# Rounds of eight edge tiles instead of batches of four in a graph-attention kernel

## The chip, the cores and the metric

One core of a Trainium2 chip. The metric is the device time of one execution in microseconds (us); lower is better. Engines: PE (matrix), DVE (vector), ACT (scalar), POOL (here it only issues gathers) and SP (issues plain transfers).

## The reference

A graph with 6250 nodes and 206250 edges, sorted by destination, with 128 features in 8 heads of 16:

```python
Qh, Kh, Vh = (h @ W).reshape(N, 8, 16)   # for WQ, WK, WV
Eh = (edge_attr @ WE).reshape(-1, 8, 16)
score = einsum('ehd,ehd,ehd->eh', Kh[src], Qh[dst], Eh) / sqrt(16)
score = exp(clip(score, -5, 5))
wV = segment_sum(Vh[src] * score[:, :, None], dst)
Z = segment_sum(score, dst)
out = layernorm(x + wV / (Z + 1e-6))
```

## The kernel before

Edges are cut into 1612 tiles of 128, one edge to a partition, and tiles into batches of four. A first stage makes a table of K and V rows (`kv`, in DRAM). Then 406 batches run through a software pipeline; the order of the instructions on each engine is the order in which the Python code issues them (a scheduler only arranges the first twelve batches).

- **Gathers (L397, POOL).** One indirect DMA for each tile fetches 128 rows of K and V by source node. The first gather of a batch carries a dependency on a matmul of an earlier batch (`expanded[b - lag(b)]`, lag from 12 batches down to 3), so that gathers keep PE's pace; the others of the batch have none.
- **Columns (L352 to L370).** For 141 tiles the rows are not gathered. ACT (104 source nodes) and DVE (24) copy the nodes' columns of x, 4 bytes in each of 128 partitions, from `xT_sb` into a tile `xcol`, one instruction for each column, its address taken from a register; a register load (L365) fetches eight addresses at once. PE projects the tile (L379), DVE puts the result in the place of the gathered rows (L386). The copies are spread over the batches by a due count (`columns`): one column tile in 2.6 batches.
- **Scores.** PE expands Q rows by a one-hot matrix (`qps`, L448) and projects edge features (`eps`, L453), one PSUM bank each. DVE multiplies K by Q (`kq`, L459), by E (`kqe`, L462), reduces by head (`sc`, L465) and clips (L468). ACT takes the exponential twice, into PSUM for DVE (`exp_p`, L474) and beside the messages (`msg`, L476). DVE multiplies V by it (L503).
- **Sums.** PE adds messages and weights into a window of 128 nodes by another one-hot matrix (`agg`, L525); two batches share a window, and two windows a PSUM tile, which ACT copies out once per four batches (`sum`, L535). Windows are shifted into blocks of 128 nodes (`finps`, L488), ACT copies these (`fin`, L498), and DVE normalizes.
- **Order in iteration b.** PE's Q and E for b; gathers; half of ACT's columns; DVE: kq(b-1), one-hot(b+2), kqe(b-1), turned one-hot(b+2), reduce(b-1), messages(b-2), DVE's columns, clip(b-1); ACT: exponentials(b-1), the rest of its columns; PE: sums(b-2).

Of the kernel before, what the change touches and what calls it, by code (L numbers as in the profile page):

```python
# [16 lines left out]
P = 128  # L17
# [3 lines left out]
B = 4  # L21
G = 4
HW = 64
HALF = 16
# [4 lines left out]
CH = 8  # L29
GB = 14  # L30
XB = 12
LOCK = XB + 6
STEP = 3
GLEAD = 2
OHB = (3, 5)
# [5 lines left out]
AHEAD = 2  # L41
EB = 6
SLAG = 2
# [8 lines left out]
COL0 = 32  # L52
COLP = (13, 5)
COLA = (8, 13)
COLV = (8, 3)
COLL = 8
RING = 4096
SUMS = 8
# [4 lines left out]
def cut_batches():  # L63
    out, t = [], 0
    while t < NT:
        k = B
        if t >= NT - TAIL:
            k = 2 if NT - t > 3 else 1
        out.append(range(t, t + k))
        t += k  # L70
    return out
# [9 lines left out]
def pair_of(t):  # L81

    return (t // (2 * G), t // G % 2) if t < LAST else (NT, 1)


def pair_start(k):

    return (2 * k * G * N + NT // 2) // NT - DRIFT


def window_start(t):
    k, half = pair_of(t)
    return QL * P + HW if k == NT else pair_start(k) + HALF * half
# [8 lines left out]
def edge_attention(ctx: ExitStack, tc: tile.TileContext, x, xT, srcT, srcC, dstT, dstB, dst0, bnd, lo, eaT,  # L102
# [26 lines left out]
    halves = [[cp.tile([P, B, P], F32, name=f"onehot{h}{i}") for i in range(OHB[h])] for h in range(2)]  # L129
# [11 lines left out]
    with ExitStack() as fast:  # L141
# [8 lines left out]
        nc.vector.tensor_scalar(shift[:HW], io_i[:HW], 0, None, op0=ALU.is_equal)  # L150
        nc.vector.tensor_scalar(shift[HW:], io_i[HW:], HALF - HW, None, op0=ALU.is_equal)
        nc.vector.tensor_scalar(ident, io_i[:, P:2 * P], 0, None, op0=ALU.is_equal)
        for h in range(2):
            for tl in halves[h]:
                nc.vector.memset(tl[:, :, HW - HW * h:P - HW * h], 0.0)
# [85 lines left out]
        psA = fast.enter_context(tc.tile_pool(name="psA", bufs=2, space=bass.MemoryType.PSUM))  # L241
        psX = fast.enter_context(tc.tile_pool(name="psX", bufs=1, space=bass.MemoryType.PSUM))

        iota_p = psX.tile([P, HW], F32, name="iota_p")
        exp_p = psX.tile([P, B, H], F32, name="exp_p")
# [33 lines left out]
        xbs, stores, norms, pending, ready, finished, loaded_x = {}, [], [], [], [], [], set()  # L279
# [39 lines left out]
        def load_rel(c):  # L319
            if c in rels or c * RC >= NT:  # L320
                return
            n = min(RC, NT - c * RC) * P
            rels[c] = wp.tile([QROWS, RC * P], BF16, name="relb", bufs=2)
# [3 lines left out]
        chunks, aggs, sums, st8, expanded = {}, {}, {}, {}, {}  # L327
# [20 lines left out]
        used = [0, 0]  # L348
# [59 lines left out]
        def project(g, n):  # L408

            pt = psT.tile([P, B, P], F32, name="xtps", tag="oT")  # L410
            for i in range(n):
                nc.tensor.transpose(pt[:, i, :], g[:, i, :D], ident)
            xgT = wp.tile([P, B, P], F32, name="xgT", tag="kq", bufs=2)
            nc.scalar.copy(xgT[:, :n], pt[:, :n])
            for i in range(0, n, 2):
                k = min(2, n - i)
                pk = pair_bank(i // 2, "kvps", [P, 2, 2 * D])
                for j in range(k):
                    nc.tensor.matmul(pk[:, j, :], xgT[:, i + j, :], wkv_sb, start=True, stop=True)  # L419
                nc.scalar.copy(g[:, i:i + k, :], pk[:, :k, :])  # L420

        def stage_0(b):
            t0, n = batches[b][0], len(batches[b])
            half = pair_of(t0)[1]
            oh = halves[half][used[half] % OHB[half]]
            used[half] += 1
            nc.vector.tensor_tensor(oh[:, :n, HW * half:HW * half + HW],  # L427
                                    iota_p[:, None, :].to_broadcast([P, n, HW]),
                                    rel[:, t0:t0 + n, None].to_broadcast([P, n, HW]), op=ALU.is_equal)
            st8[b] = oh, None  # L430

        def stage_0t(b):
            t0, n = batches[b][0], len(batches[b])
            oh = st8[b][0]
            ohT = wp.tile([QROWS, B * P], BF16, name="onehotT", bufs=AHEAD + 2)
# [3 lines left out]
            st8[b] = oh, ohT  # L439

        def stage_a(b, g):
            t0, n = batches[b][0], len(batches[b])
            if b < XB:
                project(g, n)
            oh, ohT = st8.pop(b)
            pq = psQ.tile([P, B, D], F32, name="qps")
            for i in range(n):
                expanded[b] = nc.tensor.matmul(pq[:, i, :], ohT[:, i * P:i * P + P], loaded[t0 // WT],  # L448
                                               start=True, stop=True)
            pe = psE.tile([P, B, D], F32, name="eps")  # L450
            ea = ea_tiles(t0, n)
            for i in range(n):
                nc.tensor.matmul(pe[:, i, :], ea[:, i * P:i * P + P], we_sb, start=True, stop=True)  # L453
            st8[b] = [n, g, oh, pq, pe]

        def stage_b(b):
            n, g, oh, pq, pe = st8[b]
            t0 = wp.tile([P, B, D], F32, name="kq", bufs=2)
            nc.vector.tensor_tensor(t0[:, :n], g[:, :n, :D], pq[:, :n], op=ALU.mult)  # L459
            yield  # L460
            t1 = wp.tile([P, B, D], F32, name="kqe", bufs=2)
            nc.vector.tensor_tensor(t1[:, :n], t0[:, :n], pe[:, :n], op=ALU.mult)  # L462
            yield
            sc = wp.tile([P, B, H], F32, name="sc")
            nc.vector.tensor_reduce(sc[:, :n], t1[:, :n].rearrange("p b (h d) -> p b h d", h=H),  # L465
# [3 lines left out]
            st8[b] = [n, g, oh, sc]  # L469

        def weigh(b):

            n, g, oh, sc = st8[b]
            nc.scalar.activation(exp_p[:, :n], sc[:, :n], AF.Exp, scale=0.25)  # L474
            m = wp.tile([P, B, MW], F32, name="msg")
            nc.scalar.activation(m[:, :n, D:], sc[:, :n], AF.Exp, scale=0.25)  # L476
            st8[b] = [n, g, oh, m]

        def windows(q):

            return [(k, pair_start(k) - q * P) for k in range(min(NT, LAST + 2 * G - 1) // (2 * G))
                    if -HW - HALF < pair_start(k) - q * P < P]

        def add_windows(ps, q, first, stop):

            parts = windows(q)
            for i, (k, s) in enumerate(parts):
                nc.tensor.matmul(ps, shift[:, P - s:2 * P - s], sums[k // 2][:, k % 2],  # L488
# [12 lines left out]
        def messages(b):  # L501
            n, g, oh, m = st8[b]
# [5 lines left out]
        def stage_c(b):  # L508
            n, g, oh, m = st8.pop(b)
            for i in range(n):  # L510
                t = batches[b][i]
                k, half = pair_of(t)
# [5 lines left out]
                u = k if final else k // 2  # L518
                first = u not in aggs
                if first:  # L520
                    aggs[u] = psA.tile([P, 2, MW], F32, name="agg")
                    if final:
                        add_windows(aggs[u][:, 0], QL, True, False)
                tail = k == NT if t == NT - 1 else pair_of(t + 1)[0] != k
                nc.tensor.matmul(aggs[u][:, 0 if final else k % 2], oh[:, i, :], m[:, i, :],  # L525
                                 start=not final and t % (2 * G) == 0, stop=tail)
                if tail and final:
                    norms.extend(pending)
# [3 lines left out]
                    norms.append(layernorm(nc, sp, aggs.pop(u)[:, :1], xbs.pop(QL), out, QL, 1, stores))  # L532
                elif tail and (k % 2 == 1 or t == LAST - 1):
                    sums[u] = sp.tile([P, 2, MW], F32, name="sum", bufs=SUMS)
                    nc.scalar.copy(sums[u][:, :k % 2 + 1], aggs.pop(u)[:, :k % 2 + 1])  # L535
                    while len(finished) < QL // 2 and all(v // 2 <= u for v, _ in windows(2 * len(finished) + 1)):
                        ready.append(len(finished))
                        finished.append(u)

        gathered = {b: gather(b) for b in range(2)}  # L540
        for b0 in range(0, NB, KB):
# [3 lines left out]
            for b in range(len(gathered), min(XB, nbat)):  # L545
                if (b - 2 if b < 5 else b) * KB > b0:
                    break
# [6 lines left out]
        load_rel(0)  # L554
        for j in range(QLOOK):
            load_q(j)

        def fill():

            if qwork:  # L560
# [5 lines left out]
        for b in range(nbat + 3):  # L566
# [6 lines left out]
            if b < nbat:  # L573
                load_chunk(batches[b][0] // CH + EB - 3)
                load_rel(batches[b][0] // RC + 1)
                load_q(batches[b][0] // WT + QLOOK)
                g = gathered.pop(b)
                if b == min(XB, nbat - 1):
                    late_loads()
                if b == min(XB + 8, nbat - 1):  # L580
                    relative(C0, NT)
                if b == 14:
                    from_window(1)
                if b == 0:
                    for i in range(AHEAD):
                        stage_0(i)
                        stage_0t(i)
                stage_a(b, g)
# [3 lines left out]
            norms.extend(pending)  # L592
# [4 lines left out]
            steps = stage_b(b - 1) if 0 <= b - 1 < nbat else iter(())  # L597
            next(steps, None)
            if b + AHEAD < nbat:
                stage_0(b + AHEAD)  # L600
            fill()
            next(steps, None)
            place_columns()
            if b + AHEAD < nbat:
                stage_0t(b + AHEAD)
            fill()
            next(steps, None)
            if 0 <= b - 2 < nbat:
                messages(b - 2)
# [181 lines left out]
```

## Time and profile before

| | us |
|---|---|
| median of 3 runs | 2546.33 (2535.9 to 2577.7) |
| the profiled execution | 2564.92 |
| its span | 2563.1 |
| first column copies to last, about | 250 to 2500 |

In the profile a line such as "L370 ACT COPY xcol<-xT_sb 128x4 uint8 x14664 | busy, mean ns | idle <-releaser" is a group of equal instructions: the time in which one of them runs, the mean of one, and the idle time of the engine just before them with what ended it. "issue" means that nothing the profile shows was waited for. A row of the waits reads: total us, times, longest. A row of the timeline reads: start, duration, engine, line, and in brackets the idle time before it. A row of a window reads: from and to, its length, then busy us and instruction count of each engine, then PE's granted clock, the DMA engines' share and GB/s. "remote" is a wait that a DMA's landing ended. Instructions on an engine overlap: a small copy takes 190 ns from start to acknowledged end, and the next may start 95 ns after it.

### The profile page before, as it was taken

What the parts mean: (1) busy time and instruction counts of PE and PEld (TensorE: products, weight loads), DVE (VectorE), ACT (ScalarE), POOL (GpSimd) and SP (SyncE); (2) the same over time, 40 slices, a digit from 0 to 9 for tenths busy, and PEclk for the clock granted to TensorE, in tenths of its full rate; (3) what the DMA queues carried; (4) which work ended last, traced back from release to release, by engine and by line L of the source; (5) the groups of instructions that cost most, each with busy time, mean ns of one, the idle gap of its engine ahead of it and who ended that gap; (6) DMA issues with size and microseconds to landing.
All of it is one profiled execution on the core that took longest, in us unless ns stands there. A gap on an engine that the chain in (4) does not pass through costs nothing.

```text
span 2563.1 us, 49459 instructions
## 1 busy us (share of the span) xinstructions
PE 1618.7 (63%) x9332; PEld 1406.9 (55%) x9332; DVE 1757.4 (69%) x7175; ACT 1700.3 (66%) x15663; POOL 1398.5 (55%) x1478
## 2 busy tenths in 40 slices
PE   4665555566665666666656566666666666666666
PEld 3554455455555556555555555555555565555555
DVE  2365666777767767777767677677676777767776
ACT  1221667677776777777767777777776777777771
POOL 5455445555555555555555555455555555555554
PEclk7687778776877877787777778877777677777777
DMA  6555434455455446445545454454455545545542
GB/s 204 178 157 165 136 119 148 139 164 156 135 152 162 131 132 191 131 150 156 152 147 146 144 162 129 141 176 134 136 155 156 151 131 163 163 130 150 155 144 79
DMA packets 171260, 381.43 MB, mean 149 GB/s; under 512 B 58733, under 2 KB 84645, under 8 KB 170943
## 3 DMA queue, kind: packets, MB, share of 16 engines
q0 software_dynamic: 69824, 189.69, 25.6%
q1 hardware_dynamic: 99979, 187.45, 24.1%
q14 instruction: 240, 1.97, 0.3%
q8 instruction: 77, 1.26, 0.2%
q10 hardware_dynamic: 1140, 1.06, 0.1%
HBM read 363.26 MB, written 14.81 MB: 148 GB/s over the span
## 4 chain that ended last, share of the span: by engine, by line
ACT 48%; issue 23%; DVE 9%; PE 8%; ACTq 7%; another core or an unknown queue 3%; DMA 1%; POOL 0%; DVEq 0%; SPq 0%; POOLq 0%
ACT xcol L370 44%; ACTq L365 7%; PE agg L525 2%; PE eps L453 2%; ACT msg L476 2%; DVE kqe L462 1%; DVE xcol L370 1%; DVE kq L459 1%; ACT exp_p L474 1%; DVE msg L503 1%; DVE sc L465 1%; PE kvps L419 1%; PE finps L488 1%; ACT sum L535 1%
## 5 line engine op out<-in xcount | busy, mean ns | idle before, releaser
L397 POOL DMA_INDIRECT kvrows<-kv,src x1423 | 1352.1, 950 | 1116.1 <-PE qps L448 382.1
L370 ACT COPY xcol<-xT_sb 128x4 uint8 x14664 | 1560.9, 190 | 557.3 <-issue 544.4
L525 PE MATMUL agg<-msg,onehot 128*128 128x136 f32 x3224 | 635.5, 356 | 561.2 <-DVE msg L503 406.9
L525 PEld LDWEIGHTS agg<-msg,onehot 128*128 128x128 f32 x3224 | 551.5, 250 | 621.9 <-ACT msg L476 383.2
L453 PE MATMUL eps<-we_sb,ea 128*128 128x128 f32 x3224 | 607.0, 346 | 195.6 <-DVE kqe L462 67.0
L453 PEld LDWEIGHTS eps<-we_sb,ea 128*128 128x128 f32 x3224 | 528.0, 248 | 252.9 <-DVE kqe L462 96.4
L503 DVE TENSOR_TENSOR msg<-kvrows,exp_p 128x512 f32<-128x512 f32 x406 | 275.8, 679 | 415.6 <-ACT exp_p L474 262.7
L370 DVE COPY xcol<-xT_sb 128x4 uint8 x3384 | 301.7, 194 | 16.9 <-issue 10.8
L459 DVE TENSOR_TENSOR kq<-kvrows,qps 128x512 f32<-128x512 f32 x406 | 274.2, 675 | 40.7 <-remote 24.7
L462 DVE TENSOR_TENSOR kqe<-kq,eps 128x512 f32<-128x512 f32 x406 | 273.7, 674 | 26.6 <-remote 18.2
L465 DVE TENSOR_REDUCE sc<-kqe 128x32 f32<-128x512 f32 x406 | 272.1, 670 | 0.3
L448 PE MATMUL qps<-qw,onehotT 126*128 126x128 bf16 x1612 | 200.1, 259 | 84.3 <-DVE kq L459 47.8
L448 PEld LDWEIGHTS <-onehotT 126*128 126x128 bf16 x1612 | 159.5, 120 | 153.6 <-issue 130.5
L427 DVE TENSOR_TENSOR onehot<-iota_p,dst_sb 128x256 f32<-128x256 f32 x406 | 167.9, 414 | 2.4 <-PE agg L525 2.4
L437 DVE TENSOR_SCALAR onehotT<-relb,node 126x512 bf16<-126x512 bf16 x406 | 146.3, 361 | 5.8 <-PE qps L448 2.6
L474 ACT ACTIVATE exp_p<-sc 128x32 f32<-128x32 f32 x406 | 78.0, 192 | 107.6 <-DVE sc L468 57.2
L386 DVE COPY kvrows<-colkv 128x256 f32<-128x256 f32 x141 | 59.5, 422 | 87.9 <-PE eps L453 26.3
L379 PE MATMUL colkv<-wkv_sb,xcol 128*128 128x256 f32 x282 | 115.3, 501 | 0.0
L488 PE MATMUL finps<-sum,shift 128*128 128x136 f32 x640 | 93.1, 305 | 32.7 <-ACT sum L535 29.0
L488 PEld LDWEIGHTS finps<-sum,shift 128*128 128x128 f32 x640 | 88.3, 213 | 35.7 <-ACT sum L535 31.7
L476 ACT ACTIVATE msg<-sc 128x32 f32<-128x32 f32 x406 | 86.9, 214 | 7.1 <-issue 6.6
L468 DVE TENSOR_SCALAR sc<-sc 128x32 f32<-128x32 f32 x406 | 81.8, 202 | 0.3
(72 smaller groups left out, 562.6 us busy)
## 6 DMA issues: line engine op xcount, KB each, us to landing
ea<-eaT SPq DMA_DIRECT2D x201, 512.0 KB
relb<-relD SPq DMA_DIRECT2D x100, 504.0 KB
kvrows<-kv,src POOLq DMA_INDIRECT x1423
qw<-qs SPq DMA_DIRECT2D x202, 31.5 KB
kv<-kvst SPq DMA_DIRECT2D x12, 512.0 KB
qs<-qst SPq DMA_DIRECT2D x48, 96.0 KB
xb<-x SPq DMA_DIRECT2D x24, 128.0 KB
out<-h SPq DMA_DIRECT2D x24, 128.0 KB
```

The source lines that it names most:

```text
L365: at = nc.values_load_multi_w_load_instructions(col_at[k % col_half:k % col_half + 1, k // col_half, j:j + size], engines=(engine,), min_v ...
L370: copy(to[:, 4 * (j + c):4 * (j + c) + 4], xT_bytes[:, ds(at[c] - XT_AT, 4)])
L397: ins = nc.gpsimd.indirect_dma_start(out=g[:k, i, :f], out_offset=None, in_=rows, in_offset=bass.IndirectOffsetOnAxis(ap=src_col(t)[:k], a ...
L427: nc.vector.tensor_tensor(oh[:, :n, HW * half:HW * half + HW], iota_p[:, None, :].to_broadcast([P, n, HW]), rel[:, t0:t0 + n, None].to_bro ...
L448: expanded[b] = nc.tensor.matmul(pq[:, i, :], ohT[:, i * P:i * P + P], loaded[t0 // WT], start=True, stop=True)
L453: nc.tensor.matmul(pe[:, i, :], ea[:, i * P:i * P + P], we_sb, start=True, stop=True)
L459: nc.vector.tensor_tensor(t0[:, :n], g[:, :n, :D], pq[:, :n], op=ALU.mult)
L462: nc.vector.tensor_tensor(t1[:, :n], t0[:, :n], pe[:, :n], op=ALU.mult)
L465: nc.vector.tensor_reduce(sc[:, :n], t1[:, :n].rearrange("p b (h d) -> p b h d", h=H), axis=AX.X, op=ALU.add)
L488: nc.tensor.matmul(ps, shift[:, P - s:2 * P - s], sums[k // 2][:, k % 2], start=first and i == 0, stop=stop and i == len(parts) - 1)
L503: nc.vector.tensor_tensor(m[:, :n, :D].rearrange("p b (h d) -> p b h d", h=H), g[:, :n, D:].rearrange("p b (h d) -> p b h d", h=H), exp_p[ ...
L525: nc.tensor.matmul(aggs[u][:, 0 if final else k % 2], oh[:, i, :], m[:, i, :], start=not final and t % (2 * G) == 0, stop=tail)
```

## The change

Batches become rounds of eight tiles (206 instead of 406). Each round's Q and E are made and used in two halves of four tiles, with two PSUM banks for each (they come from `agg`, which goes from two banks to one, and from putting the one-hots' iota and the exponentials into one). Reduction, clip, both one-hots, exponentials and messages are done for eight tiles at once. The sums' window spans sixteen tiles instead of eight, with the one-hot written at one of four offsets; ACT copies one window out per two rounds. Column tiles come one per 1.25 rounds: 144 of them, with eight addresses to a load as before. kq and kqe of a half follow each other on DVE, kqe in place. The one-hot for the sums is made in its own round, ahead of the clip, from a ring of three. Gathers: eight per round, buffers for 8 rounds (14 batches before), first gather of a round tied to the matmul `lag` rounds before (6 down to 2).

```diff
-B = 4
+B = 8
-GB = 14
-XB = 12
+GB = 8
+XB = 6
-STEP = 3
-GLEAD = 2
+STEP = 2
+GLEAD = 1
-COLP = (13, 5)
+COLP = (5, 4)
...
-        psE = fast.enter_context(tc.tile_pool(name="psE", bufs=1, space=bass.MemoryType.PSUM))
-        psQ = fast.enter_context(tc.tile_pool(name="psQ", bufs=1, space=bass.MemoryType.PSUM))
+        psE = fast.enter_context(tc.tile_pool(name="psE", bufs=2, space=bass.MemoryType.PSUM))
+        psQ = fast.enter_context(tc.tile_pool(name="psQ", bufs=2, space=bass.MemoryType.PSUM))
...
         def lag(b):
-            return max(STEP, 12 - (b - LOCK) // 40)
+            return max(STEP, 6 - (b - LOCK) // 20)
...
+            nc.vector.tensor_tensor(t0[:, a:e], g[:, a:e, :D], pq[:, :k], op=ALU.mult)
             yield
+            nc.vector.tensor_tensor(t0[:, a:e], t0[:, a:e], pe[:, :k], op=ALU.mult)
...
+        def take_sums():
+            for k in closed:
+                sums[k] = sp.tile([P, MW], F32, name="sum", bufs=SUMS)
+                nc.scalar.copy(sums[k], agg[:, k % 2])
...
+            for _ in stage_b(b, 0):
+                fill()
+            stage_a(b + 1, 0)
+            fill()
+            take_sums()
+            if 0 <= b - 1 < nbat:
+                messages(b - 1)
+            fill()
+            place_columns()
+            if b < nbat:
+                columns(nc.vector, b, 0.5)
+            for _ in stage_b(b, 1):
+                fill()
+            stage_a(b + 1, 1)
+            if 0 <= b - 1 < nbat:
+                stage_c(b - 1)
+            steps = stage_s(b) if b < nbat else iter(())
             next(steps, None)
+            turned_one_hots(b + 2)
+            if b < nbat:
+                one_hots(b)
             fill()
             next(steps, None)
+            if b < nbat:
+                weigh(b)
             fill()
             if b < nbat:
                 columns(nc.vector, b)
+                columns(nc.scalar, b)
```

`stage_a` is PE's Q and E for a half, `stage_b` DVE's two products, `stage_s` reduction and clip, `weigh` the exponentials, `stage_c` PE's sums. ACT's other half of the columns of round b stands ahead of all this.

More of the change, by code (lines that the diff above doesn't have):

```diff
@@ L408, in project @@
         def project(g, n):
[L410 to L420, printed above, removed]
@@ L422, in stage_0 @@
-        def stage_0(b):
+            for a in range(0, n, G):
+                h = min(G, n - a)
+                pt = psT.tile([P, G, P], F32, name="xtps", tag="oT")
+                for i in range(h):
+                    nc.tensor.transpose(pt[:, i, :], g[:, a + i, :D], ident)
+                xgT = wp.tile([P, G, P], F32, name="xgT", tag="kvst", bufs=2)
+                nc.scalar.copy(xgT[:, :h], pt[:, :h])
+                for i in range(0, h, 2):
+                    k = min(2, h - i)
+                    pk = psT.tile([P, 2, 2 * D], F32, name="kvps", tag="oT")
+                    for j in range(k):
+                        nc.tensor.matmul(pk[:, j, :], xgT[:, i + j, :], wkv_sb, start=True, stop=True)
+                    nc.scalar.copy(g[:, a + i:a + i + k, :], pk[:, :k, :])
@@ L456, in stage_b @@
[L456 to L459, printed above, removed]
-            yield
[L461 to L465, printed above, removed]
+            st8[b] = [ohT]
@@ new lines, in half, with stage_a @@
+        def half(b, h):
+            return range(h * G, min(len(batches[b]), h * G + G)) if 0 <= b < nbat else range(0)
+        def stage_a(b, h):
+            own = half(b, h)
+            if not own:
+                return
+            if b < XB and h == 0:
+                project(gathered[b], len(batches[b]))
+            t0, ohT = batches[b][0], st8[b][0]
+            pq = psQ.tile([P, G, D], F32, name="qps")
+            for i in own:
+                expanded[b] = nc.tensor.matmul(pq[:, i - own[0], :], ohT[:, i * P:i * P + P], loaded[t0 // WT],
+                                               start=True, stop=True)
+            pe = psE.tile([P, G, D], F32, name="eps")
+            ea = ea_tiles(t0, len(batches[b]))
+            for i in own:
+                nc.tensor.matmul(pe[:, i - own[0], :], ea[:, i * P:i * P + P], we_sb, start=True, stop=True)
+            st8[b].append((pq, pe))
@@ L517, in stage_c @@
                 final = k == NT
[L518 to L526, printed above, removed]
-                if tail and final:
-                    norms.extend(pending)
+                u = (LAST - 1) // (QUAD * G) + 1 if final else k
+                if final and t == LAST:
+                    take_sums()
+                    add_windows(agg[:, u % 2], QL, True, False)
+                tail = t == NT - 1 or window_of(t + 1)[0] != k
+                nc.tensor.matmul(agg[:, u % 2], oh[:, i * P + HW - at:][:, :P], m[:, i, :],
+                                 start=not final and t % (QUAD * G) == 0, stop=tail)
+                if tail and final:
+                    for j in ready:
+                        finish(j)
+                    ready.clear()
+                    norms.extend(waiting + pending)
+                    waiting.clear()
                     pending.clear()
@@ L531, in stage_c @@
                         fill()
[L532 to L540, printed above, removed]
+                    norms.append(layernorm(nc, sp, agg[:, u % 2:u % 2 + 1], xbs.pop(QL), out, QL, 1, stores))
+                elif tail:
+                    closed.append(k)
+        def take_sums():
+            for k in closed:
+                sums[k] = sp.tile([P, MW], F32, name="sum", bufs=SUMS)
+                nc.scalar.copy(sums[k], agg[:, k % 2])
+                while len(finished) < QL // 2 and all(v <= k for v, _ in windows(2 * len(finished) + 1)):
+                    ready.append(len(finished))
+                    finished.append(k)
+            closed.clear()
+        gathered = {0: gather(0)}
         for b0 in range(0, NB, KB):
@@ L565, in edge_attention @@
         held = []
-        for b in range(nbat + 3):
+        for b in range(nbat + 2):
+            now[0] = b
             if b >= XB and not manual:
```

174 lines of the change are left out of this document (79 added, 95 removed).

## The prediction

> **What bounds the kernel now.** I began with the page: span, busy shares, and the chain of work that ended last.
>
> ```profile
> span 2563.1 us, 49459 instructions
> PE 1618.7 (63%) x9332; PEld 1406.9 (55%) x9332; DVE 1757.4 (69%) x7175; ACT 1700.3 (66%) x15663; POOL 1398.5 (55%) x1478
> ACT 48%; issue 23%; DVE 9%; PE 8%; ACTq 7%; another core or an unknown queue 3%; DMA 1%; POOL 0%; DVEq 0%; SPq 0%; POOLq 0%
> L397 POOL DMA_INDIRECT kvrows<-kv,src x1423 | 1352.1, 950 | 1116.1 <-PE qps L448 382.1
> L370 ACT COPY xcol<-xT_sb 128x4 uint8 x14664 | 1560.9, 190 | 557.3 <-issue 544.4
> ```
>
> By busy shares nothing is full (DVE leads with 69%), but the chain runs through ACT and "issue". ACT's column copies (L370) keep it busy 1560.9 us, and before them it idles another 557 us, 544 of which waited for no other engine. So I asked what ACT waits for in the stretch in which columns are copied (about 250 to 2500 us), and how busy the engines are there.
>
> ```profile
> ACT xcol L370 <- issue: 544.1, 1008, 1.2
> ACT exp_p L474 <- issue: 13.9, 22, 1.2
> ACT exp_p L474 <- DVE sc L468: 5.2, 4, 3.7
> ACT fin L498 <- PE finps L488: 4.9, 3, 2.7
> ACT sum L535 <- PE agg L525: 1.1, 1, 1.1
> 250.00:2500.00 2250.00, 1427.61 (x8291) 1248.09 (x8291) 1598.88 (x6756) 1651.41 (x15497) 1231.85 (x1297) 0.77 0.50 148
> ```
>
> The last row gives PE, weight loads, DVE, ACT and POOL. ACT is busy 1651 us and held up in issue 570 (544.1, 13.9 and two rows of 6.6 and 5.9): 2222 of 2250 us. It waits for DVE and PE some 11 us in all. ACT is full; everyone else waits for it. The 570 us are worth understanding, so I laid POOL's timeline beside ACT's.
>
> ```profile
> 1072.70 0.94 POOL L397 DMA_INDIRECT kvrows<-kv,src  x1 [1.87 <-remote]
> 1075.20 0.95 POOL L397 DMA_INDIRECT kvrows<-kv,src  x1 [0.30 <-issue]
> ...
> 1080.30 0.95 POOL L397 DMA_INDIRECT kvrows<-kv,src  x1 [0.30 <-issue]
> 1086.40 0.95 POOL L397 DMA_INDIRECT kvrows<-kv,src  x1 [5.16 <-DVE kqe L462]
> ```
>
> ```profile
> 1072.65 0.19 ACT L474 ACTIVATE exp_p<-sc 128x32 f32<-128x32 f32 x1
> 1072.78 0.21 ACT L476 ACTIVATE msg<-sc 128x32 f32<-128x32 f32 x1
> 1072.90 2.51 ACT L370 COPY xcol<-xT_sb 128x4 uint8 x24
> 1075.32 0.38 ACT L535 COPY sum<-agg 128x272 f32<-128x272 f32 x1
> 1075.59 0.95 ACT L370 COPY xcol<-xT_sb 128x4 uint8 x9
> 1076.94 0.38 ACT L370 COPY xcol<-xT_sb 128x4 uint8 x3 [0.39 <-issue]
> 1077.71 0.19 ACT L370 COPY xcol<-xT_sb 128x4 uint8 x1 [0.38 <-issue]
> ...
> 1081.25 0.38 ACT L370 COPY xcol<-xT_sb 128x4 uint8 x3 [0.50 <-issue]
> 1082.67 3.52 ACT L370 COPY xcol<-xT_sb 128x4 uint8 x36 [1.04 <-issue]
> ```
>
> A train of seven gathers, 1.25 us apart, starts at 1072.70; its third gather starts at 1075.20. ACT copies at 0.1 us each (24 in 2.51 us) until shortly after that, then 1 to 3 copies between gaps of 0.4 to 1.0 us. The train's last gather ends at 1081.25; from 1082.67 ACT runs free, 36 copies in 3.52 us. I read the stalls as belonging to the third and later gathers of a train. Trains of other lengths test that; these are ACT's issue waits within three windows.
>
> ```profile
> ACT xcol L370 <- issue: 1.7, 2, 1.1
> ACT xcol L370 <- issue: 4.1, 8, 1.0
> ACT xcol L370 <- issue: 5.1, 9, 1.1
> ```
>
> They are a train of four (1091.0 to 1097.1 us), the seven above (1072.7 to 1086.4) and a train of eight (1579.1 to 1594.4). Per gather past the second: 1.7/2 = 0.85, 4.1/5 = 0.82, 5.1/6 = 0.85. The law 0.84 x (n - 2) can be held against the whole stretch: POOL's timeline there has 335 trains with 1295 gathers, so 1295 - 670 = 625 gathers past the second, 525 us; measured 544. Short trains are nearly free now because each batch of four tiles opens its own: POOL's first gather of a batch waits for PE.
>
> [...]
>
> **The change, part by part.** Counts for the changed kernel come from its built instruction list.
>
> *Trains of gathers.* POOL now waits once per round of eight tiles; the instruction list has one wait for PE and DVE ahead of the first gather, then 8 gathers, or 7 where a column tile takes the place of one. 144 column tiles (141 before) lie in about 180 rounds: 144 trains of seven and 36 of eight. Stalls: 144 x 4.1 + 36 x 5.1 = 774 us against 544: **+230**. This is the main term. [...] These rows hold ACT's column copies alone:
>
> ```profile
> 1072.70:1086.40 13.70, 8.80 (x82) 0.50 0.25 71
> 1579.10:1594.40 15.30, 8.52 (x79) 0.77 0.46 140
> ```
>
> A round copies 104 x 0.8 = 83 columns, what these windows hold. At 13.7 us with seven gathers and 15.3 with eight, 180 rounds take 144 x 13.7 + 36 x 15.3 = 2524 us for the stretch's 2250: +274.
>
> *Column copies.* 14976 instead of 14664: 312 x 0.106 us (1560.9/14664) = **+33**, on ACT, on the path.
>
> *Exponentials.* 206 pairs instead of 406, 64 elements wide instead of 32. A pair costs 0.25 us (1072.65 to the copy at 1072.90). An element costs what wide copies differ by:
>
> ```profile
> L414 ACT COPY xgT<-xtps 128x512 f32<-128x512 f32 x12 | 7.0, 584 | 37.5 <-remote 18.5 <-PE xtps L412 16.0 <-PE eps L453 2.7
> L535 ACT COPY sum<-agg 128x272 f32<-128x272 f32 x100 | 37.7, 377 | 37.5 <-remote 23.3 <-PE agg L525 6.9 <-issue 5.9
> L535 ACT COPY sum<-agg 128x136 f32<-128x136 f32 x1 | 0.3, 272 | 0.3 <-PE agg L525 0.3
> ```
>
> (584 - 377)/240 = 0.86 ns, so 32 more elements twice are 0.055 us. -200 x 0.25 + 206 x 0.055 = **-39**. *Sums over sixteen tiles:* 101 copies of 136 instead of 272: 101 x (0.377 - 0.272) = **-11**.
>
> *DVE.* Reduction, clip, both one-hots and messages become 200 to 206 instructions of twice the width; kq and kqe stay 406. That saves fixed costs off the path: 14648 copies at 40 a batch (104/2.6) are 366 batches of 6.15 us, DVE is busy 1599/366 = 4.4 us in each, so at most 8.7 us per eight tiles where ACT needs 13.8. kq and kqe now follow each other directly, and so do kqe and the reduction; each may wait for its forerunner's write, at most the 0.19 us that a whole small copy takes (ACT's row, 190 ns), 0.8 us a round, hidden by the 5 us to spare. DVE's own columns (3456 copies, 19 a round) now fall inside long trains too. If they stall as ACT's do, 3 copies in 1.42 us (1081.25 to 1082.67), in the 7.5 of 13.7 us from a seven-train's third gather to 1 us after its last, they take 0.55 x 19 x 0.47 + 0.45 x 19 x 0.1 = 5.8 instead of 1.9 us: DVE 12.6, still under ACT's round. If all did, 9 us, DVE 15.8 and the round 2 us longer.
>
> *PSUM in pairs.* E and Q of the next half can be made while DVE reads this half. ACT waited 4.9 us for PE's window matmuls and hardly at all else, so PE being ahead gains nothing while ACT is full. *Window matmuls* (finps) fall from 640 records to 370, on PE, off the path. *The sum's copy* now stands ahead of the exponentials in ACT's queue; behind it wait the exponentials, and DVE's messages wait for these. PE's last matmul of a window is issued in the round before, and of 101 sums one waited for it so far, 1.1 us: I take zero; its other end, 1.1 us each, is 111. *SP* gets relb three deep and ea one chunk earlier; none of ACT's waits names a transfer: zero. *Start-up and end* (250 and 63 us): same tiles, same engines; zero, 20 either way, twice the longest single wait for a landing there (9.3 us):
>
> ```profile
> DVE kq L459 <- remote: 17.4, 3, 9.3
> ```
>
> Sum: 2563 + 230 + 33 - 39 - 11 = 2776 us of span. The profiled execution took 2564.9 us, 18.6 above the median 2546.3; taken off like that, the forecast is 2776 + 2 - 19, about **2760**. Upper ends: +274 for the trains gives 2803, and the start-up's 20 and DVE's 2 us in one round of seven (52) on top 2875; the sums' 111 alone 2871.
>
> **Rivals.**
> 1. *One stall for each round (faster).* In the timeline above the stalls begin some 4 us after the exponentials as well as after a train's opening; if the toll is per train or per hand-over between DVE and ACT, it halves: 180 x 1.7 = 306, and 2563 - 238 - 17 = 2308, median 2290. DVE's 8.7 us per eight tiles (1566 for 180 rounds) would allow it, and POOL's 8 x 1.25 too. For it: the usual four-trains fit a fixed toll. Against it: 4.1 and 5.1 us in single long trains. 0.11.
> 2. *Stalls go with the copies (no change).* [...] Gaps then grow by 2%: 544 x 312/14664 = 12; 2563 + 12 + 33 - 39 - 11 = 2558, and up to 28 us of ACT's remaining waits can go: 2530 to 2558, median 2512 to 2540. Against it: free copying before the third gather and after the last. 0.08.
> 3. *The trains break up.* Each gather also waits for the one eight before it; should that or the free buffers (8 of eight tiles) hold POOL after three or four gathers, the change doesn't lengthen trains and the time is that of rival 2. For it: nothing in the trace; 1.25 us x 8 is longer than a gather takes to land. 0.06.
>
> **Chances.** 0.75 for the forecast. From no change I count about 2% as told apart (the three runs spread over 1.6%). Faster by over 2% only rival 1, with a little of 2: 0.12; within 2%: 0.13; slower: 0.75. The forecast's own range is 2660 to 2875 (below: half of the 230 gone, since the law rests on 28 long trains). To hold 8 in 10, the range reaches down to 2505 for rivals 2 and 3, leaving out rival 1 and some 0.06 above 2875.
>
> **What would show it.** Right: POOL's timeline shows seven or eight gathers 1.25 us apart once in 13 to 14 us; "ACT xcol <- issue" in the waits near 770 us; ACT busy plus issue again nearly the whole stretch; the longest wait of DVE is messages for the exponentials. Wrong: issue waits at or under 550 us with long trains (rivals 1, 2), trains of four (rival 3), or ACT waiting for DVE or PE for more than 100 us, which would be a bound that I don't see.

## The result and the profile after

The changed kernel takes 2758.2 us (median of four runs, 2755.0 to 2762.9); the kernel before took 2545.5 us beside it (2535.9 to 2577.7). The ratio is 1.082, with a 95% interval of 1.079 to 1.085. One thing has to be known for all that follows: there were two conditions, one in the runs above and in experiments 1 to 4 (the kernel before at 2536 to 2588 us), another in the eight runs of experiments 5 and 6 (1875 to 1882 us); the chip of experiments 1 to 4 also ran experiment 5, another chip experiment 6. So every experiment is held against the kernel before of its own set.

The page of the changed kernel: span, busy times, the chain that ended last, and the groups of instructions that matter.

```profile
span 2761.0 us, 47348 instructions
PE 1491.0 (54%) x9066; PEld 1324.5 (48%) x9066; DVE 1707.6 (62%) x6247; ACT 1719.2 (62%) x15575; POOL 1404.8 (51%) x1475
...
ACT 46%; issue 25%; DVE 9%; PE 8%; ACTq 6%; another core or an unknown queue 4%; DMA 1%; DVEq 1%; POOL 0%; SPq 0%; POOLq 0%
...
L369 ACT COPY xcol<-xT_sb 128x4 uint8 x14976 | 1601.0, 189 | 683.8 <-issue 671.9
```

ACT is still the longest chain, and its issue waits ahead of the column copies have grown from 544 to 672 us. POOL's timeline shows the round, one train of seven:

```profile
1191.45 0.94 POOL L396 DMA_INDIRECT kvrows<-kv,src  x1 [5.00 <-DVE kq L471]
1192.69 1.00 POOL L396 DMA_INDIRECT kvrows<-kv,src  x1 [0.30 <-issue]
...
1199.00 0.95 POOL L396 DMA_INDIRECT kvrows<-kv,src  x1 [0.30 <-issue]
1205.08 0.94 POOL L396 DMA_INDIRECT kvrows<-kv,src  x1 [5.13 <-DVE kq L471]
```

The trains are there: seven gathers, then the next train 13.6 us after the first. ACT's timeline behind the train that opens at 1205.08 shows the stalls again:

```profile
1201.33 7.19 ACT L369 COPY xcol<-xT_sb 128x4 uint8 x73 [0.44 <-issue]
1208.42 0.22 ACT L485 ACTIVATE bank<-sc 128x64 f32<-128x64 f32 x1
1208.58 0.24 ACT L487 ACTIVATE msg<-sc 128x64 f32<-128x64 f32 x1
1208.73 0.87 ACT L369 COPY xcol<-xT_sb 128x4 uint8 x6
1210.02 0.38 ACT L369 COPY xcol<-xT_sb 128x4 uint8 x3 [0.43 <-issue]
1210.76 0.38 ACT L369 COPY xcol<-xT_sb 128x4 uint8 x3 [0.36 <-issue]
1211.49 0.19 ACT L369 COPY xcol<-xT_sb 128x4 uint8 x1 [0.35 <-issue]
...
1215.04 6.35 ACT L369 COPY xcol<-xT_sb 128x4 uint8 x61 [0.51 <-issue]
```

73 copies run freely until 1208.5, across the opening of the third gather, and 6 more behind the exponentials; from 4.5 us after the train's opening they come in ones to threes between gaps; from 1215.0 they run freely again.

The whole span can be booked on ACT, between its first and its last column copy: busy time from the windows, issue and other waits from the waits in that window (some 10 us of gaps too short for the view are missing). This table also holds the experiments that are told below.

| kernel (kernel before beside it) | first copy at | stretch | busy | issue | other waits | behind the last copy |
|---|---|---|---|---|---|---|
| before (2546) | 245.8 | 2254.1 | 1653.1 | 570.8 | 19.4 | 63.2 |
| after (2546) | 232.5 | 2427.6 | 1676.1 | 696.4 | 42.3 | 100.9 |
| before, trains doubled (2564) | 253.4 | 2615.2 | 1688.3 | 850.9 | 67.5 | 67.1 |
| after, half the columns (2564) | 239.2 | 2044.9 | 930.0 | 684.1 | 423.9 | 110.8 |
| before (1879) | 172.1 | 1635.9 | 1576.1 | 28.0 | 22.1 | 65.7 |
| after (1879) | 169.3 | 1732.0 | 1578.7 | 38.1 | 107.9 | 88.2 |
| after, clip first (1879) | 171.2 | 1666.2 | 1576.9 | 36.6 | 46.1 | 91.7 |
| after, fixed addresses (1879) | 168.6 | 1622.9 | 1509.2 | 0.0 | 112.9 | 98.3 |

In the first condition the span's 198 us are: start -13, issue +126, busy +23, waits for others +23, behind the last copy +38.

### The profile page after: what moved, and what is told of

It is laid out like the page before. It is cut to its first block, busy times and chain, and to the rows that moved or that the text cites. A ratio compares the mean times of both kernels' runs of the same rounds, so it can differ in the third digit from the quotient of the medians.

```text
span 2761.0 us, 47348 instructions
## 1 busy us (share of the span) xinstructions
PE 1491.0 (54%) x9066; PEld 1324.5 (48%) x9066; DVE 1707.6 (62%) x6247; ACT 1719.2 (62%) x15575; POOL 1404.8 (51%) x1475
## 3 DMA queue, kind: packets, MB, share of 16 engines
q0 software_dynamic: 69680, 189.30, 24.0%
q10 hardware_dynamic: 1140, 1.06, 0.1%
## 4 chain that ended last, share of the span: by engine, by line
ACT 46%; issue 25%; DVE 9%; PE 8%; ACTq 6%; another core or an unknown queue 4%; DMA 1%; DVEq 1%; POOL 0%; SPq 0%; POOLq 0%
ACT xcol L369 43%; ACTq L364 6%; PE agg L535 4%; DVE sc L476 2%; ACT msg L487 1%; DVE kq L471 1%; DVE kq L469 1%; DVE xcol L369 1%; PE eps L457 1%; ACT bank L485 1%; PE colkv L378 1%; PE kvacc L262 1%; ACT sum L554 1%; DVE onehot L425 1%
## 5 line engine op out<-in xcount | busy, mean ns | idle before, releaser
L457 PE MATMUL eps<-we_sb,ea 128*128 128x128 f32 x3224 | 562.9, 327 | 91.3 <-DVE kq L471 66.3
L457 PEld LDWEIGHTS eps<-we_sb,ea 128*128 128x128 f32 x3224 | 486.1, 230 | 138.6 <-PE qps L452 60.5
L514 DVE TENSOR_TENSOR msg<-kvrows,bank 128x1024 f32<-128x1024 f32 (+2 forms) x206 | 246.0, 1194 | 429.2 <-ACT bank L485 169.0
L471 DVE TENSOR_TENSOR kq<-kq,eps 128x512 f32<-128x512 f32 x406 | 277.0, 682 | 35.4 <-remote 6.6
L476 DVE TENSOR_REDUCE sc<-kq 128x64 f32<-128x1024 f32 (+2 forms) x206 | 246.4, 1196 | 9.5 <-DVE kq L471 2.8
L425 DVE TENSOR_TENSOR onehot<-bank,dst_sb 128x512 f32<-128x512 f32 (+2 forms) x206 | 138.3, 671 | 0.0
L485 ACT ACTIVATE bank<-sc 128x64 f32<-128x64 f32 (+2 forms) x206 | 45.9, 223 | 120.5 <-DVE sc L479 67.1
L435 DVE TENSOR_SCALAR onehotT<-relb,node 126x1024 bf16<-126x1024 bf16 (+2 forms) x206 | 99.6, 484 | 1.0 <-PE qps L452 1.0
L378 PEld LDWEIGHTS colkv<-wkv_sb,xcol 128*128 128x128 f32 x288 | 57.0, 241 | 0.8 <-DVE qr L292 0.5
L396 POOL DMA_INDIRECT kvrows<-x,src x48 | 45.8, 953 | 21.8 <-issue 13.7
```

Of the source, the lines that this page charges most:

```text
L378: nc.tensor.matmul(pk, col_tiles.pop(k), wkv_sb, start=True, stop=True)
L396: ins = nc.gpsimd.indirect_dma_start(out=g[:k, i, :f], out_offset=None, in_=rows, in_offset=bass.IndirectOffsetOnAxis(ap=src_col(t)[:k], a ...
L425: nc.vector.tensor_tensor(onehots[b % OHB][:, HW:].rearrange("p (t n) -> p t n", n=P)[:, :n, :HW], iota_p[:, None, :].to_broadcast([P, n, ...
L457: nc.tensor.matmul(pe[:, i - own[0], :], ea[:, i * P:i * P + P], we_sb, start=True, stop=True)
L471: nc.vector.tensor_tensor(t0[:, a:e], t0[:, a:e], pe[:, :k], op=ALU.mult)
L476: nc.vector.tensor_reduce(sc[:, :n], t0[:, :n].rearrange("p b (h d) -> p b h d", h=H), axis=AX.X, op=ALU.add)
```

## The experiments

**1. Are long trains what stalls ACT?** In the kernel before, only every second batch's gathers wait for PE:

```diff
-                if i == 0 and b >= LOCK:
+                if i == 0 and b >= LOCK and b % 2 == 0:
```

> The kernel before, where only every second batch's gathers wait for PE, so that two batches' gathers follow each other: trains of six to eight, and everything else as it was. Theory of the trains: at what the changed kernel's trains cost (3.6 us for seven, 4.4 for eight) 180 trains make 677 us of issue waits instead of 544, and the time becomes about 2680; at the law of the prediction (0.84 us for each gather past the second) 774 us and about 2775. Rivals: no change, 2545 within 30.

It took 2938 us, 1.143 (1.136 to 1.150) of the kernel before. There are 135 trains of seven and 42 of eight in the stretch of the column copies, and ACT waits:

```profile
ACT xcol L370 <- issue: 794.7, 1339, 1.2
ACT fin L498 <- remote: 51.8, 11, 7.3
ACT exp_p L474 <- issue: 29.4, 53, 1.1
ACT msg L476 <- issue: 23.1, 43, 1.1
```

795 us ahead of the column copies, instead of 544: the same copies, the same bytes, only the grouping of the gathers differs. Between a train's opening and the next one lie 4.1 us of stalls for seven and 5.4 for eight. The law's 774 us of stalls thus came true, its 2775 us of time did not: beside the 250 us of stalls of the copies there are 30 us more of other issue waits, 48 of waits for others and 35 of busy time.

**2. The same from the other side, first try.** In the changed kernel the fifth gather of a round gets a wait of its own, for the first half's query matmul of the batch after:

```diff
-                if i == 0 and made is not None:
+                if i == G and b >= LOCK:
+                    made = expanded[b - lag(b) + 1, 0]
+                if i in (0, G) and made is not None and (i == 0 or b >= LOCK):
```

> The changed kernel, with the train of gathers cut in the middle: the fifth gather of a round waits for the first half's query matmul of the batch after the one that the first gather waits for. POOL should show trains of three and four. Theory of the trains (a long train stalls ACT's copies more than two short ones): ACT's issue waits ahead of the column copies fall from 665 us by 100 to 200, and the time by as much, to 2560 to 2660. Rivals, by which the stalls go with the copies or with the hand-over to ACT once a round: issue waits stay within 40 us of 665 and the time within 30 us of 2758.

2881 us, 1.122 (1.115 to 1.129). It doesn't answer the question: 131 trains of seven and 35 of eight are left, nearly those of the changed kernel. It came out slower still than that (1.082), with 768 us of issue and 99 us of waits for others in ACT's stretch: a train of seven costs 4.1 us here and 3.6 in the changed kernel, so the length of a train alone doesn't set its price. What else does wasn't followed up.

**3. Is it the loading of the addresses?** In the changed kernel each engine loads eight addresses once:

```diff
-                at = nc.values_load_multi_w_load_instructions(
+                if engine not in addresses:
+                    addresses[engine] = nc.values_load_multi_w_load_instructions(
...
+                at = addresses[engine]
```

> The changed kernel, where each of ACT and DVE loads its eight addresses from SBUF once and uses them for all columns: the copies still take their address from registers, the later loads are left out (the columns are then the wrong nodes'). If the copies themselves are slow beside a train of gathers, issue waits stay at 665 us within 60 and the time within 40 of 2758. If the stalls hang on the loads of the registers, which fetch from SBUF while POOL's gathers run, issue waits fall below 150 us, ACT is no longer full, and the time falls to what POOL or DVE allow: POOL's round of seven gathers 1.25 us apart with some 1 us at its wait is 10 to 11 us, 200 of them with 300 us ahead and behind give 2300 to 2500.

2740 us, 1.066 (1.059 to 1.073). Issue waits ahead of ACT's column copies are 693 us: only two register loads are left on ACT in this trace, so it isn't the loads, the copies themselves are held up.

**4. Is ACT what is full, and do the stalls go with the copies?** Half as many column tiles in the changed kernel, `COLP = (5, 2)` for `(5, 4)`:

> The changed kernel with half as many column tiles (one in 2.5 rounds instead of one in 1.25). If ACT is what is full, its copies fall by 800 us and the bound goes over to POOL: some 7.6 gathers at 1.25 us and about 1 us at the wait are 10.6 us a round, 200 rounds with 300 us ahead and behind 2420: 2380 to 2520, faster than both kernels. If DVE, PE or the hand-overs of the new round set its pace of 13.7 us, the time stays above 2650.

2397 us, 0.932 (0.927 to 0.938) of the kernel before: faster than both. ACT is no longer full (424 us of waits for others). Half the copies keep most of the stalls (568 of 672 us, with 72 more tiles to gather), which therefore don't go with the copies:

```profile
ACT xcol L369 <- issue: 568.0, 998, 1.9
ACT bank L485 <- DVE sc L479: 116.7, 29, 6.3
```

Whether the gain on the kernel before comes from the rounds or from fewer columns alone is not shown: in this condition the kernel before wasn't run with half the columns.

**5. Trains cut in the middle, second try; fixed addresses; half the bytes; the kernel before with half the columns.** In this set the kernel before took 1878 us, and the numbers expected for the other condition can't be met; what remains are comparisons within it. The first three are edits of the changed kernel, which itself takes 1999.8 us in this condition (experiment 6, another set and chip).

```diff
+                if eng is nc.scalar:
+                    acted[b] = ins
...
+                if i == G and b >= LOCK:
+                    made = acted.get(b - lag(b) - 1)
```

> The changed kernel, with the train cut by another event than in the first try (there the fifth gather's matmul had been done when its turn came, and 124 trains of seven were left): the fifth gather now waits for ACT's last column copy of an earlier round, which stands about 8 us behind the opening of the train. POOL should show trains of three and four instead of seven and eight. Theory of the trains: what such trains cost in the kernel before (0.84 us for three, 1.68 for four) gives 144 x 2.5 + 36 x 3.4 = 482 us of issue waits ahead of ACT's copies instead of 672, and the time 2570 within 50. If what counts is the number of gathers and not their bunching, issue waits stay within 50 of 672 and the time at 2758 or above it, since POOL now also waits for ACT.

2005 us, 1.068 (1.067 to 1.070). The trains weren't cut here either: only six of three or four stand in the stretch, and rows of 14 and 15 gathers are as common as sevens, as in the changed kernel in this condition, where POOL catches up and the trains run into each other. With issue waits of 39.7 us (38.1 without the edit) there was little to be had. That shorter trains relieve ACT in the changed kernel is thus shown by no run; experiment 1 shows the other direction.

```diff
-                    copy(to[:, 4 * (j + c):4 * (j + c) + 4], xT_bytes[:, ds(at[c] - XT_AT, 4)])
+                    copy(to[:, 4 * (j + c):4 * (j + c) + 4],
+                         xT_bytes[:, 4 * (LEFT + 8 * k + c):4 * (LEFT + 8 * k + c) + 4])
```

> The changed kernel, where the column copies read from addresses written in the program; the eight addresses are still loaded into registers, but no copy uses them (the columns are then the wrong nodes'). If a copy stalls because its address comes from a register, issue waits ahead of ACT's copies fall from 672 us below 150, and the time falls to what POOL and DVE allow, 2300 to 2500. If any small copy of ACT stalls beside a train of gathers (its reads and writes of SBUF, or its instruction stream), issue waits stay at 672 within 80 and the time within 50 of 2758.

1890 us, 1.007 (1.005 to 1.009), and 1890 again in the third set. With addresses in the program ACT's issue waits are 0.0 (38.1 with registers), and DVE's column copies lose theirs too (0.4 us; 50.7 in the changed kernel). The larger part of the 110 us gained is busy time, 69 us less on ACT. The expectation has one thing wrong: the loads did not stay. The trace has one register load on ACT (1873 in the changed kernel), so the edit takes away loads and register addresses together, and this run can't tell which of them the 38 us belong to. In the first condition it wasn't run.

```diff
-            rows, f = (x, D) if b < XB else (kv, 2 * D)
+            rows, f = (x, D)
```

Every gather fetches the 512-byte rows of x instead of the 1024-byte rows of the table, so half the bytes (96.27 MB on the gathers' queue instead of 189.30); keys and values are then x itself.

> [...] If ACT's copies stall on the bytes that the gathers bring into SBUF, issue waits fall from 672 us towards half, 340, and the time to 2430 or less. [...]

1998 us, 1.064 (1.063 to 1.066): the changed kernel's time. With 38.7 us of stalls to begin with, this says nothing on what causes them.

The kernel before with `COLP = (26, 5)` for `(13, 5)`:

> The kernel before with half as many column tiles (one in 5.2 batches instead of 2.6). Half the columns made the changed kernel 2397 us. If the change's own gain is that POOL waits once in eight tiles and not once in four, this kernel goes over to POOL's bound with twice as many waits of some 1 us: 3.8 gathers at 1.25 us and 1.05 are 5.8 us a batch, 400 batches with 300 us ahead and behind 2620, within 80: slower than before, and some 200 us slower than the changed kernel with as few columns. If fewer columns are the whole of the gain there, this kernel comes to 2400 as well.

1961 us, 1.044 (1.042 to 1.045): slower than with all columns. POOL is now the bound: in the stretch of the column copies 1373 of 1375 gathers start 0.3 us after the end of the one before, without a pause for waits. ACT's column copies, half as many, wait 122.5 us for issue, where all of them waited 28.0 in the kernel before: a little stalling is left in this condition too, 122.5 us over 1375 gathers or about 0.09 us a gather. So half the columns cost the kernel before 4% here; whether experiment 4's gain would survive here wasn't tried.

**6. Both kernels in the second condition, and the clip.** The repeats of experiment 5's fixed addresses and of both kernels ran beside the clip's edit:

```diff
             next(steps, None)
+            next(steps, None)
+            if b < nbat:
+                weigh(b)
             turned_one_hots(b + 2)
             if b < nbat:
                 one_hots(b)
             fill()
-            next(steps, None)
-            if b < nbat:
-                weigh(b)
             fill()
...
-                                    iota_p[:, None, :].to_broadcast([P, n, HW]),
+                                    iota_f[:, None, :HW].to_broadcast([P, n, HW]),
```

> The changed kernel as it is, beside the kernel before. The sets of runs so far found the chip in two conditions, told apart by the kernel before: 2546 to 2564 us, and 1878 us with hardly any issue waits. If it stands at 2550 again, 2758 within 40 and issue waits of some 670 us ahead of ACT's copies. If it stands at 1878: were the stalls the whole of the loss, the changed kernel would come to 1878 within 30; but its sister with half the bytes a gather took 1998 there, with 39 us of issue waits and 109 us in which ACT waited for DVE's scores, so by a theory of the lost lead (the exponentials stand in the round whose scores they need, a round earlier than before) 1970 to 2010.

> The kernel before as it is, for its profile in the same condition. At 2550: 544 us of issue waits within 40 and some 11 us of ACT's waits for DVE and PE. At 1878: by the theory of the lost lead ACT waits under 30 us for DVE there too, against some 110 in the changed kernel; if ACT waits as long here, the lost lead falls as a cause.

> The changed kernel with the clip back in front of both one-hots (1.15 us of DVE's work by the means of 671 and 484 ns), so that scores reach ACT that much sooner; so that the exponentials don't wait for the one-hots after all, these read the row of numbers from SBUF and not from the PSUM bank which the exponentials write. By the theory of the lost lead ACT's waits for DVE shrink by up to 1.15 us each: with the kernel before at 1878, from 110 to about 30 us and the time by 60 to 100; at 2550, from 33 to about 10 and the time by 20 to 50. If the waits for the scores are not what counts, the time stays within 15 of the changed kernel's.

> The changed kernel with copies from addresses written in the program, once more. With the kernel before at 2550: if the stalls belong to copies that take their address from a register, issue waits fall from 672 us below 60 and the time below 2350; if to any small copy of ACT, issue waits stay above 500 and the time above 2600. At 1878 it repeats 1890 within 10.

The changed kernel: 1999.8 us, 1.065 (1.063 to 1.067). So it is slower here too, but with 10 us more of issue waits instead of 126. ACT's waits in its column stretch, of the changed kernel and then of the kernel before:

```profile
ACT bank L485 <- DVE sc L479: 74.0, 51, 4.8
ACT xcol L369 <- issue: 38.1, 154, 0.5
ACT bank L485 <- DVE y L770: 27.1, 17, 2.3
ACT bank L485 <- DVE st L759: 6.6, 4, 2.6
```

```profile
ACT xcol L370 <- issue: 28.0, 107, 0.5
ACT exp_p L474 <- DVE sc L468: 13.3, 16, 5.4
ACT fin L498 <- PE finps L488: 5.5, 7, 1.1
```

The exponentials wait 108 us for DVE's scores, where those before waited 16. (Rows that name `y` and `st`, steps of the layer norm, are waits of the same exponentials.) Of the 116 us of span, 86 are waits of ACT for others, 10 issue, 3 busy; the start gives 3 back, and 22 lie behind the last copy (short gaps give the remaining 2 back). With the clip ahead of the one-hots (and ahead of one step of the layer norm that `fill` puts there) the time falls to 1934 us, 1.030 (1.028 to 1.032), and the waits to 46 us; the one-hots take 669 ns from SBUF as from PSUM. More than half of the loss in this condition is thus the order of these few instructions.

The timelines show the loop in which they stand. PE, ACT and DVE of the changed kernel in one round:

```profile
1035.56 3.99 PE L535 MATMUL agg<-msg,onehot 128*128 128x136 f32 x16 [2.47 <-ACT sum L554]
1039.35 1.06 PE L378 MATMUL colkv<-wkv_sb,xcol 128*128 128x256 f32 x2
```

```profile
1035.25 0.26 ACT L554 COPY sum<-agg 128x136 f32<-128x136 f32 x1
1035.41 0.22 ACT L485 ACTIVATE bank<-sc 128x64 f32<-128x64 f32 x1
1035.57 0.24 ACT L487 ACTIVATE msg<-sc 128x64 f32<-128x64 f32 x1
1035.71 8.93 ACT L369 COPY xcol<-xT_sb 128x4 uint8 x88
1044.55 0.38 ACT L509 COPY fin<-finps 128x272 f32<-128x272 f32 x1
1045.92 0.23 ACT L485 ACTIVATE bank<-sc 128x64 f32<-128x64 f32 x1 [0.99 <-DVE sc L479]
```

```profile
1040.44 0.42 DVE L385 COPY kvrows<-colkv 128x256 f32<-128x256 f32 x1 [3.44 <-PE colkv L378]
1041.37 0.76 DVE L369 COPY xcol<-xT_sb 128x4 uint8 x8 [0.50 <-issue]
1041.94 0.68 DVE L469 TENSOR_TENSOR kq<-kvrows,qps 128x512 f32<-128x512 f32 x1
...
1043.38 1.22 DVE L476 TENSOR_REDUCE sc<-kq 128x64 f32<-128x1024 f32 x1
1044.51 0.48 DVE L435 TENSOR_SCALAR onehotT<-relb,node 126x1024 bf16<-126x1024 bf16 x1
1044.90 0.68 DVE L425 TENSOR_TENSOR onehot<-bank,dst_sb 128x512 f32<-128x512 f32 x1
1045.51 0.32 DVE L479 TENSOR_SCALAR sc<-sc 128x64 f32<-128x64 f32 x1
```

PE's messages matmuls wait 2.47 us for ACT's copy of the sum; the column tile's projection stands behind them; DVE waits 3.44 us for that projection before it can go on to the second half, the reduction, both one-hots and the clip; and then ACT, out of copies, waits 0.99 us for the clip. From the sum's copy to these exponentials it is 10.7 us, more than ACT has work for. This happens once in two rounds, as a window closes: 96 of the 108 us fall to the second exponentials after a sum's copy, as here. DVE's waits for the projection are 128.2 us here and 10.2 in the kernel before.

PE's clock is a further link of this loop. The same work one round earlier, and the two stretches (PE's granted clock stands third from the end):

```profile
1024.30 2.02 PE L535 MATMUL agg<-msg,onehot 128*128 128x136 f32 x16
1026.16 0.59 PE L378 MATMUL colkv<-wkv_sb,xcol 128*128 128x256 f32 x2
```

```profile
1024.00:1026.30 2.30, 2.30 (x22) 2.30 (x21) 2.30 (x13) 2.30 (x25) 1.69 (x3) 1.00 1.01 306
1035.56:1039.50 3.94, 3.94 (x17) 3.94 (x18) 1.44 (x2) 3.94 (x41) 3.03 (x4) 0.50 0.39 118
```

At a granted clock of 0.50 the sixteen matmuls take 3.99 us instead of 2.02 and the projection 1.06 instead of 0.59: 2.4 us more, where ACT waits 0.99. In 84 of the 89 rounds in which a window closes these matmuls take over 3 us, at a mean clock of 0.52, and nearly all of the 96 us lie in them; with the clip first it is 66 of 89, and 28.5 of 29.0 us. That the clip's place costs is shown by the run; that PE's wait for the sum starts the loop, and how much of it the slower clock makes, is read from these rows and was not tried alone.

## Why the prediction held, and where its steps failed

*ACT is full; more stalls make the kernel slower.* Held. Busy and issue are 1676 + 696 of 2428 us, and with half the columns the same kernel drops to 2397 us.

*Stalls belong to long trains: +230 us.* The mechanism held, the size did not: +128 ahead of the copies (+126 over all of ACT). The trains came as counted, 142 of seven, 35 of eight and one of sixteen, and in the old kernel with doubled trains the law was good: 774 us by it, 795 measured, and 4.1 us for a train of seven as in the prediction. But in the changed kernel a train of seven costs 3.6 us and one of eight 4.5. ACT's first gap opens there 3.8 us behind a seven-train's opening in the median, in the doubled kernel before 3.3; between 3 and 4 us after the opening of a train of seven or eight ACT still makes 7.0 copies, there 3.4. Why it begins later stayed open.

*Rival 1, one toll for each round.* Fell: longer trains cost more, in both kernels. *Rival 2, stalls go with the copies.* Fell by experiments 1 and 4. A column copy itself takes 190 ns in the mean both with 795 us of issue waits ahead of the copies (experiment 1) and with none (fixed addresses); what is late is its issue, and in the second condition ACT's issue waits go from 38.1 us to 0.0 when the copies take their address from the program (and the loads of the registers are gone with it). *Rival 3, broken trains.* Fell: 177 of the 178 trains are of seven or eight. By the packets of the gathers' queue a gather has landed 2.5 us after its start in the median and 7.4 at most (7.8 in the kernel before), less than 8 x 1.25 us.

*Copies +33, exponentials -39, sums -11: together -17 on ACT.* ACT's busy time rose by 23 us. Exponentials and sums saved 33 and 11 us of it, near the forecast; what was missing is on the column copies, which took 67 us more of ACT's time instead of 33 (each instruction booked from the end of the one before). The 312 more copies are 30 of these. A further part comes from the stalls: a copy in a row takes 0.095 us, the last one before a gap its whole 0.19, and ACT's busy time falls into 1495 pieces instead of 1236, some 25 us more by estimate. In the doubled kernel before, with the same instructions, 353 more pieces make 34 of its 35 us in the same way. The prediction priced a stall by its gap alone.

*The sum's place in ACT's queue: zero, with 111 as the other end. DVE hidden, with 5 us a round to spare.* These are the steps that failed. They compared busy times and the old waits, not the loop that closes within a round. With the stalls on ACT its waits for others rose by 23 us; without them by 86 of 116, near the end that wasn't taken. DVE's own columns, which the prediction let stall as ACT's do (3.9 us a round), lost 71 us in all, 0.4 a round. The sign that the prediction named, ACT waiting over 100 us for DVE or PE, doesn't show in the first condition (42) and does in the second (108).

*Start and end: zero, 20 either way.* The start gave 13 us back, the end took 38. `column_tiles` stops four batches from the end, which is now 32 tiles instead of 16, and a round ahead is twice as long: by the records of the sums' matmuls (two a tile) 86 tiles are left behind the last column copy, 56 before.

That the forecast of 2760 meets 2758 so closely is luck: the stalls were 104 us and the start 13 too high, the end, the loop and the busy time 38, 23 and 40 us too low, which leaves the span 15 us too long (2776 against 2761); and the 19 us taken off because the profiled run lay above the median were 5 in the changed kernel. And it holds for the condition in which its profile was taken: beside a kernel before at 1879 us the stalls are 10 of 116 us, and the change loses 6.5% to what was set to zero.

## What to carry to other kernels

Busy time to spare doesn't hide a step that lies on a loop between engines (in the second condition DVE was busy 1519 of 1732 us here, and ACT still waited 108 us for its scores): follow the loop from a result to the next use of the same buffer, count everything queued ahead in it on every engine, and set that against the full engine's work in one round. In this kernel the larger rounds made such a loop longer (DVE's waits for the column projection: 128.2 us, 10.2 before) and the waits of the paced queue rarer (206 rounds for 406 batches), so work that was balanced for the old rounds (the column copies that relieved POOL) has to be balanced again. Look at the granted clock within the loop, too: a mean of 0.80 over the run hid that PE was granted 0.50 just there. A stall can belong to a condition of the chip and not to the kernel: the same kernel before had 544 us of issue waits ahead of its copies in one set of runs and 28 in another, so look at the same kernel twice before building on it.

## What the hardware showed unexpectedly

The kernel before took 2564 us in the first set of experiments and 1878 in the next, without a change in it. A gather's pitch stayed at 1.25 us and a column copy's duration at 190 ns. What differed: ACT's issue waits ahead of register-addressed copies (544 and 28 us), the granted TensorE clock of the profiled runs (0.77 and 0.94), and SP's register moves, of which 46 of 184 took over 100 ns in the first trace (mean 133) and none in the second (29). A train of seven gathers holds such copies up for 3.6 us (changed kernel) to 4.1 (doubled trains) in the first condition; in the second, beside 519 gathers in a row, half as many copies waited 45 us for issue, about 0.09 a gather. What the chip was doing in the first stays open.
